# Layer-norm square sums moved to VectorE, reciprocals read from PSUM, and neighbour sums queued ahead of the tail steps

## The chip, the cores and the metric

The kernel runs on one core of one Trainium2 chip. The metric is the device time of one execution in microseconds, as the median of the runs; lower is better. TensorE does matmuls (PE in the profile, its weight loads PEld), VectorE is DVE, ScalarE is ACT, GpSimd is POOL, SyncE is SP. Each engine works through its own queue in the order of the program; between engines there are only semaphores.

## The reference

Four graph layers run one after the other over 16 graphs that share one adjacency matrix of 1024 nodes, with 128 features for each node. An entry of the matrix is set with probability 0.0078, so a node has some 8 neighbours. Layers L0, L2 and L3 are masked attention with 8 heads of 16 features and a feed-forward block; L1 is a graph attention with one score for each edge.

```python
# L0, L2, L3
scores = einsum('bnhd,bmhd->bhnm', h @ Wq, h @ Wk) / 4, -inf where adj == 0
x = h + softmax(scores) @ (h @ Wv) @ Wo + bo
x = layer_norm(x) * ln1_g + ln1_b
y = relu(x @ W1 + b1) @ W2 + b2
x = layer_norm(x + y) * ln2_g + ln2_b
# L1
h = x @ W;  e = leaky_relu(h @ a_src (of the row) + h @ a_dst (of the neighbour))
x = layer_norm(softmax(e, -inf where adj == 0) @ h + x)
# layer_norm(v) = (v - mean(v)) * rsqrt(var(v) + 1e-5), over the 128 features
```

## The kernel before

A preparation sorts the nodes by degree and makes lists of neighbours; a dense path for graphs that do not fit the lists is in the program and is not run here. After the preparation the work is 64 **units**: layer (4) by group of 8 graphs (2) by block of 128 nodes (8). A unit has **parts**: in an attention layer a part is up to two gathers from the table of keys and values (`gathered`, L841, indirect DMAs from POOL), five parts in most units and seven in the first block of a group. A unit of L1 has three or four parts of up to four gathers.

For each part of an attention unit VectorE does three passes over some 2048 elements in each partition: P, query times key (`products`, L868); R, the sum over the 16 features of a head (`exponentials`, L891, after which ScalarE takes the exponential, L895); and W, value times exponential (`weighted`, L919). W is for the part before, P and R are for the current one. Then TensorE adds the edges' rows into an accumulator in PSUM (`summed`, L935), two iterations after P, and this gives P's buffer free (tile `pr`, four buffers). The last part of a unit (input `qx`) has half the elements, so its P and R are short.

After a unit's last part, `divided` (L963) adds up the exponentials in a PSUM bank (`den`), ScalarE copies that to `both`, VectorE takes the reciprocal (L973) and multiplies it into the accumulator for each half of the 8 graphs (L976, tile `o`). This starts two **tails**, one for each half block of 4 graphs (`attention_tail` L631, `graph_tail` L674), the second one step behind the first. A tail is a generator: each `yield` ends a step. An attention tail goes: transpose `o`; multiply by Wo into PSUM (`yps`); normalise; transpose with gain and shift (`turned`, L600, tile `x`); W1 and relu (L655, L659); W2 into PSUM (L664, L668); normalise; transpose; project to the next layer's keys and values, or put out.

`normed` (L575) is the normalisation. The mean has been taken out by the weights, so only the square sum is needed. In one step ScalarE squares each of the 4 graphs' 128 columns out of PSUM and accumulates each one's sum in `total` (L580, 4 instructions with an accumulator); in the next, POOL raises `total` to the power -0.5 (L586); in the next, ScalarE scales each graph's columns (L589).

The order is written out by hand (`manual_schedule`, the loop from L1055). An iteration is one part: P; `others()`; `summed` of two parts back, and at a unit's end the first half of `divided`; R and the exponential; `others()`; W of the part before and a gather; at a unit's end all tail steps that are left and the second half of `divided`; `others()`. One `others()` (L1003) advances all tails by a step, as often as a pace says, and one step of preparing the next unit (`fronts`: queries, L823 and L831; or loads). The pace is STEPS (15) or GRAPH_STEPS (8) over the number of calls in the unit. So what stands in `others()` ahead of the exponential in the program stands ahead of it in ScalarE's queue too.

Of the kernel before, what the change touches and what calls it, by code (L numbers as in the profile page):

```python
# [15 lines left out]
AF = mybir.ActivationFunctionType  # L16
ALU = mybir.AluOpType
# [4 lines left out]
D = 128  # L22
# [23 lines left out]
GH = G // HF  # L46
# [59 lines left out]

STEPS = 15
GRAPH_STEPS = 8  # L110
EDGES = 4
AHEAD = 4

# [9 lines left out]
def sparse_path(ctx: ExitStack, tc: tile.TileContext, a: dict, out: bass.AP, flag):  # L123


    nc = tc.nc
# [6 lines left out]
    def bank(shape):  # L133
        return banks.tile(shape, F32, tag="ps", name="ps")
# [22 lines left out]
    root = const.tile([P, 1], F32, name="root")  # L157
# [24 lines left out]
    def gather_buffer():  # L182
        return gathers.tile([P, max(4 * ROW, J * (ROW + G))], F32, tag="e", name="e")
# [391 lines left out]
    def normed(y):  # L575

        z = twos.tile([P, GH, D], F32, tag="o", name="z")
        total = smalls.tile([P, GH], F32, tag="total", name="total")
        for i in range(GH):
            nc.scalar.activation(  # L580
                z[:, i, :], y[:, i, :], AF.Square, scale=D**-0.5, bias=root,
                accum_out=total[:, i : i + 1],
            )
        yield
        rstd = smalls.tile([P, GH], F32, tag="rstd", name="rstd")
        nc.gpsimd.tensor_tensor(rstd, total, power, ALU.pow)  # L586
        yield
        for i in range(GH):
            nc.scalar.activation(z[:, i, :], y[:, i, :], AF.Copy, scale=rstd[:, i : i + 1])  # L589
        return z  # L590
# [178 lines left out]
    def is_attention(u):  # L769
        return LAYERS[units[u][0]][1] is ATTN  # L770
# [157 lines left out]
    def marked(t, chunk, outs, rhss):  # L928

        j, r = chunk  # L930
        for mark, j in (
            [(MARK[t, j, r], j)] if j < J else [(MARK[t, MIX, k], SHARED[t][k]) for k in range(2)]
        ):
            last = (MIX, 0) if j in SHARED[t] else (j, COUNT[t][j] - 1)
            nc.tensor.matmul(  # L935
                outs[32 * j : 32 * j + 32], marks[:, mark, :], rhss,
                start=(r == 0 and chunk[0] != MIX), stop=(chunk == last),
            )
# [24 lines left out]
    def divided(u):  # L963

        l, g, t = units[u]
        heads, d = (H, HD) if is_attention(u) else (1, D)
        den = bank([P, G * heads])
        for n, c in enumerate(sum(PIECES[t], [])):
            marked(t, c, den, exs[u][:, n, :])
        both = smalls.tile([P, 2, G * heads], F32, tag="both", name="both")  # L970
        nc.scalar.copy(both[:, 0, :], den)
        yield
        nc.vector.reciprocal(both[:, 1, :], both[:, 0, :])  # L973
        for h in range(HF):
            o = twos.tile([P, GH, D], F32, tag="o", name="o")
            nc.vector.tensor_tensor(  # L976
                o.rearrange("p g (a d) -> p (g a) d", d=d),
                accums[u][:, h, :].rearrange("p (a d) -> p a d", d=d),
                both[:, 1, h * GH * heads : (h + 1) * GH * heads]
                .rearrange("p (a o) -> p a o", o=1)  # L980
                .to_broadcast([P, GH * heads, d]),
                ALU.mult,
            )
            tails.append((attention_tail if heads > 1 else graph_tail)(l, g, t, h, o))
        n = G * heads
        nc.gpsimd.tensor_tensor(seen[:, :, :n], seen[:, :, :n], both, ALU.add)

# [5 lines left out]
    def advance(gens):  # L993
        for gen in list(gens):
            if next(gen, "end") == "end":
                gens.remove(gen)
# [3 lines left out]
    def idle():  # L1000
        return slow if held[0] or not busy[0] else []

    def others():  # L1003
        pace[0] += pace[1]
        while pace[0] >= 1.0:
            advance(tails)
            pace[0] -= 1.0
        for gens in (fronts or loads or idle(),):
            if not gens:
                continue  # L1010
            got = next(gens[0], "end")
            if got == "end":
                gens.pop(0)
            if got == "idle":
                advance(idle())

    with tc.manual_schedule():
        wide = [gather_buffer() for _ in range(EDGES)]
        setup, entry, weights = graph(wide), at_once(0), load_weights("L0")
        next(setup)  # L1020
        next(weights)
        next(entry)
        more = [weights, load_graph_weights()]
        rest = slots()
        for i, room in enumerate(setup):
            if i == T:
                for gen in more:
                    next(gen)
            if room == "load":
                for _ in loaded(0):  # L1030
                    next(entry, None)
            elif room == "queries":
                for _ in entry:
                    pass
                for _ in queries(0):
                    pass
            elif isinstance(room, str):
                next(rest)
            else:
                for _ in range(room):  # L1040
                    next(entry, None)
        for _ in entry:
            pass
        scratch.close()
        prods = ctx.enter_context(tc.tile_pool(name="prods", bufs=4))
        smalls = ctx.enter_context(tc.tile_pool(name="smalls", bufs=3))
        slow.append(at_leisure(1))
        for i in range(AHEAD - 1):
            gathered(i)
        nc.gpsimd.memset(wide[3], 0.0)  # L1050
        gathered(AHEAD - 1)
        fronts.extend([rest, loaded(1)] + more)
        closing = None
        begun = 0
        for i in range(len(parts) + 2):  # L1055
            here = i < len(parts)
            u = parts[i][0] if here else len(units)
            if here:
                l = units[u][0]
                if i and parts[i - 1][0] != u:  # L1060
                    begun = i
                    if l + 1 < len(LAYERS) and LAYERS[l + 1][1] is ATTN:
                        if units[u][1:] == (0, 1):
                            more = load_weights(LAYERS[l + 1][0])
                            next(more)
                            next(more)
                        if units[u][1:] == (0, 4):
                            next(more, None)
                if is_attention(u):
                    products(i)  # L1070
            others()
            if i > 1:
                summed(i - 2)
                done = parts[i - 2][0]
                if parts[i - 1 : i] == [] or parts[i - 1][0] != done:
                    closing = divided(done)
                    next(closing)
            if here:
                exponentials(i)
            if here and i == begun + 1:  # L1080
                if is_attention(u):
                    shared(u)
                while loads:
                    advance(loads)
                if u + 1 < len(units):
                    fronts.append(queries(u + 1))
                loads.append(loaded(u + 2))
                if units[u + 2 : u + 3] and units[u + 2][0]:
                    advance(loads)
            others()  # L1090
            if 0 < i <= len(parts):
                weighted(i - 1, 0)
                if not is_attention(parts[i - 1][0]):
                    others()
                    weighted(i - 1, 2)
                gathered(i - 1 + AHEAD)
            if closing is not None and here:
                while tails:
                    advance(tails)
                for _ in closing:  # L1100
                    pass
                closing = None
                passes = 3 if is_attention(u) else 4
                steps = STEPS if is_attention(done) else GRAPH_STEPS
                pace[:] = 0.0, steps / (passes * sum(part[0] == u for part in parts) - 1)
            others()
            if i + 1 >= len(parts) or parts[i + 1][0] != u:

                while fronts:
                    advance(fronts)  # L1110
        while tails:
            advance(tails)
        for _ in closing:
            pass
        while tails:
            advance(tails)
# [434 lines left out]
```

## Time and profile before

| | |
|---|---|
| runs | 2607.16, 2613.10, 2613.42 us; median 2613.1 us |
| the profiled execution's own time | 2568.43 us |
| its span from the first to the last instruction | 2566.7 us |
| mean granted TensorE clock | 0.914 |
| DMA moved | 636.07 MB, mean 248 GB/s |

The profile shows one execution. Its page gives the busy time of each engine, the span in 40 slices, and groups of instructions: line, engine, operation, output and inputs by name, shapes, count, busy time in us, mean ns of one, and the idle time of the engine just ahead of them with what ended it. The view of waits sums that idle time by who waited for whom: us in total, times, the longest. The timeline lists instructions by start time with their length; equal instructions that follow each other are one row with their count, and brackets hold the idle time before the row and who ended it. The profiled execution is 44.7 us shorter than the median of the runs.

Counting units by their reciprocal L973, the first stands at 189.8 us, L0 lasts to about 837 us, L1 to about 1182 us, L2 and L3 follow, and the last reciprocal is at 2525.3 us. Unit 42 (L2), from 1656.77 to 1695.74 us, is looked at closely below.

### The profile page before, as it was taken

The numbers are of one execution on the slowest core, as the hardware profiler recorded it, in microseconds if no ns is written. First come the engines' busy times: TensorE is split into PE (matmuls) and PEld (weight loads), VectorE is DVE, ScalarE is ACT, GpSimd is POOL, SyncE is SP. The second block draws the span as 40 slices with busy tenths as digits, with TensorE's granted clock in tenths as the row PEclk, the third lists the DMA queues.
The fourth block names the chain that finished last, engine by engine and source line by source line (L and its number), as shares of the span: only waits on it lengthen the run. The fifth ranks groups of instructions, "written<-read, shape, count | busy, mean of one in ns | idle before, by whom it ended". The sixth has DMA issues, their size and how long they took to land. (4 is left out here: it accounts for less than half of the span.)

```text
span 2566.7 us, 36698 instructions
## 1 busy us (share of the span) xinstructions
PE 2105.7 (82%) x13124; PEld 1297.6 (51%) x13124; DVE 1931.2 (75%) x1470; ACT 1480.3 (58%) x4640; POOL 1454.9 (57%) x978
## 2 busy tenths in 40 slices
PE   6558888788887898888788888988888787788776
PEld 5425655545554554454455554555555444455444
DVE  7887687587878476567887879888797787877781
ACT  3226676566665554455476666666666565556654
POOL 3335555356665688685554556555565565566561
PEclk8679999899988999999899999999999898889898
DMA  7656777567767598888787877778776767576750
GB/s 242 240 178 235 280 274 276 201 229 256 244 246 243 175 338 305 283 308 298 275 280 246 293 254 268 262 264 294 258 262 249 249 215 259 198 245 223 255 191 18
DMA packets 168463, 636.07 MB, mean 248 GB/s; under 512 B 38328, under 2 KB 41144, under 8 KB 119774
## 3 DMA queue, kind: packets, MB, share of 16 engines
q0 software_dynamic: 92672, 485.09, 53.7%
q1 hardware_dynamic: 75600, 148.55, 17.3%
q8 instruction: 105, 1.72, 0.3%
q14 instruction: 86, 0.70, 0.1%
HBM read 603.11 MB, written 92.34 MB: 271 GB/s over the span
## 5 line engine op out<-in xcount | busy, mean ns | idle before, releaser
L856 POOL DMA_INDIRECT e<-table,idx x600 | 961.3, 1602 | 580.0 <-DVE pr L919 355.3
L919 DVE TENSOR_TENSOR pr<-e,ex 128x2048 f32<-128x2048 f32 (+1 forms) x336 | 689.8, 2061 | 161.8 <-ACT ex L895 138.5
L868 DVE TENSOR_TENSOR pr<-e,qr 128x2048 f32<-128x2048 f32 x204 | 461.1, 2260 | 152.5 <-PE acc L935 85.3
L891 DVE TENSOR_REDUCE sc<-pr 128x128 f32<-128x2048 f32 (+1 forms) x252 | 518.5, 2058 | 8.6
L586 POOL TENSOR_TENSOR rstd<-total,power 128x4 f32<-128x4 f32 x224 | 327.8, 1465 | 326.2 <-ACT z L580 312.5
L935 PE MATMUL acc<-pr,marks 128*32 128x512 f32 x2656 | 487.0, 610 | 31.1 <-DVE pr L919 31.1
L580 ACT ACTIVATE z<-yps,root 128x128 f32<-128x128 f32 x896 | 317.7, 376 | 124.1 <-PE yps L668 68.0
L596 PE MATMUL ps<-ident,z 128*128 128x128 f32 x896 | 208.0, 334 | 162.1 <-ACT z L589 161.6
L589 ACT ACTIVATE z<-yps,rstd 128x128 f32<-128x128 f32 x896 | 255.9, 378 | 92.2 <-POOL rstd L586 89.3
L596 PEld LDWEIGHTS ps<-ident,z 128*128 128x128 f32 x896 | 134.0, 157 | 346.1 <-ACT z L589 251.0
L655 PE MATMUL ps<-x,W 128*128 128x512 f32 x384 | 247.9, 781 | 32.3 <-ACT x L600 32.3
L659 ACT ACTIVATE f<-ps,b 128x512 f32<-128x512 f32 x192 | 132.2, 690 | 232.6 <-PE ps L655 232.5
L664 PE MATMUL yps<-W,f 128*128 128x128 f32 x1536 | 256.5, 285 | 11.2 <-ACT f L659 8.5
L538 PE MATMUL ps<-Wkv,xT 128*128 128x256 f32 x768 | 223.4, 425 | 32.4 <-ACT xT L600 26.7
L935 PEld LDWEIGHTS acc<-pr,marks 128*32 128x32 f32 x2656 | 100.5, 110 | 280.2 <-issue 224.8
L664 PEld LDWEIGHTS yps<-W,f 128*128 128x128 f32 x1536 | 211.4, 196 | 56.1 <-ACT f L659 37.2
L831 ACT COPY qr<-ps 128x512 f32<-128x512 f32 x384 | 196.6, 600 | 53.4 <-PE ps L828 52.9
L580 ACT ACTIVATION_READ_ACCUMULATOR z<-yps,root 128x1 f32 x896 | 193.4, 216 | 0.0
L538 PEld LDWEIGHTS ps<-Wkv,xT 128*128 128x128 f32 x768 | 146.1, 208 | 80.3 <-ACT xT L600 44.6
L644 PE MATMUL yps<-Wo,oT 128*128 128x128 f32 x768 | 159.2, 290 | 6.0 <-ACT oT L598 6.0
L645 PE MATMUL yps<-centre,x 128*128 128x128 f32 x768 | 156.6, 286 | 6.4
L542 ACT COPY kv<-ps 128x512 f32<-128x512 f32 x176 | 103.6, 590 | 89.7 <-PE ps L538 86.1
(159 smaller groups left out, 2644.4 us busy)
## 6 DMA issues: line engine op xcount, KB each, us to landing
table<-kv SPq DMA_DIRECT2D x88, 512.0 KB, 10.6
qx<-qr SPq DMA_DIRECT2D x96, 256.0 KB, 9.4
kept<-xT SPq DMA_DIRECT2D x96, 256.0 KB, 5.0
x<-kept SPq DMA_DIRECT2D x48, 512.0 KB, 9.1
e<-table,idx POOLq DMA_INDIRECT x600, 8.1
table<-kv SPq DMA_DIRECT2D x32, 256.0 KB, 11.0
edges<-in_adj SPq DMA_DIRECT2D x8, 512.0 KB, 4.9
spare<-in_x SPq DMA_DIRECT2D x8, 512.0 KB, 6.6
```

The source lines that it names most:

```text
L538: nc.tensor.matmul(ps[:, k, :], x[:, i + k, :], w[LAYERS[l][0], "Wkv"], start=True, stop=True,)
L580: nc.scalar.activation(z[:, i, :], y[:, i, :], AF.Square, scale=D**-0.5, bias=root, accum_out=total[:, i : i + 1],)
L586: nc.gpsimd.tensor_tensor(rstd, total, power, ALU.pow)
L589: nc.scalar.activation(z[:, i, :], y[:, i, :], AF.Copy, scale=rstd[:, i : i + 1])
L596: nc.tensor.transpose(ps[:, i, :], z[:, i, :], ident)
L655: nc.tensor.matmul(ps, p["W1"][:, f * P : (f + 1) * P], x1.rearrange("p g n -> p (g n)"), start=True, stop=True,)
L664: nc.tensor.matmul(ps[:, i, :], f1[:, f, i * P : (i + 1) * P], p["W2"][:, f, :], start=(f == 0), stop=False,)
L856: nc.gpsimd.indirect_dma_start(out=es[i][:, k, :], out_offset=None, in_=tables[l, g][:, :], in_offset=bass.IndirectOffsetOnAxis(ap=idx[:, ...
L868: nc.vector.tensor_tensor(prs[i][0][:, :n, :], es[i][:, :n, :ROW], qx[u].rearrange("p (o c) -> p o c", o=1) if (MIX, 0) in piece else of_p ...
L891: nc.vector.tensor_reduce(sc[:, :n, :], prs[i][0][:, :n, :].rearrange("p k (a d) -> p k a d", d=HD), mybir.AxisListType.X, ALU.add,)
L919: nc.vector.tensor_tensor(prs[i][k0 // 2][:, :m, :].rearrange("p k (a d) -> p k a d", d=d), es[i][:, k0 : k0 + m, base : base + ROW].rearr ...
L935: nc.tensor.matmul(outs[32 * j : 32 * j + 32], marks[:, mark, :], rhss, start=(r == 0 and chunk[0] != MIX), stop=(chunk == last),)
```

## The change

- `normed`: the four squares with an accumulator become one ScalarE instruction over 512 columns, which only squares. One more step is added, and after it VectorE adds up `z` over the features into `total` (128 x 4). The power on POOL comes in the same step as VectorE's sum. STEPS becomes 17 and GRAPH_STEPS 9, for the longer tails.
- `divided`: the reciprocal reads `den` in PSUM. ScalarE's copy of `den` to `both`, which only the check `seen` on POOL still needs, moves to the end.
- The loop: `summed` and the first half of `divided` come before the first `others()` of an iteration, not after it.

Lines of the changed kernel are a few lower: L580 becomes L579 (square), the new VectorE sum is L582, L586 is L584, L589 is L587, L891 is L889, L919 is L917, L935 is L933, L973 is L970, L971 is L982.

```diff
-STEPS = 15
-GRAPH_STEPS = 8
+STEPS = 17
+GRAPH_STEPS = 9
...
         total = smalls.tile([P, GH], F32, tag="total", name="total")
-        for i in range(GH):
-            nc.scalar.activation(
-                z[:, i, :], y[:, i, :], AF.Square, scale=D**-0.5, bias=root,
-                accum_out=total[:, i : i + 1],
-            )
-        yield
+        nc.scalar.activation(z, y, AF.Square, scale=D**-0.5, bias=root)
+        yield
+        yield
+        nc.vector.tensor_reduce(total, z, mybir.AxisListType.X, ALU.add)
         rstd = smalls.tile([P, GH], F32, tag="rstd", name="rstd")
         nc.gpsimd.tensor_tensor(rstd, total, power, ALU.pow)
         yield
...
         both = smalls.tile([P, 2, G * heads], F32, tag="both", name="both")
-        nc.scalar.copy(both[:, 0, :], den)
-        yield
-        nc.vector.reciprocal(both[:, 1, :], both[:, 0, :])
+        yield
+        nc.vector.reciprocal(both[:, 1, :], den)
...
             tails.append((attention_tail if heads > 1 else graph_tail)(l, g, t, h, o))
+        nc.scalar.copy(both[:, 0, :], den)
         n = G * heads
         nc.gpsimd.tensor_tensor(seen[:, :, :n], seen[:, :, :n], both, ALU.add)
...
-            others()
             if i > 1:
                 summed(i - 2)
                 done = parts[i - 2][0]
                 if parts[i - 1 : i] == [] or parts[i - 1][0] != done:
                     closing = divided(done)
                     next(closing)
+            others()
             if here:
                 exponentials(i)
```

## The prediction

> **What bounds the kernel now.** First the page's busy shares: no engine is full, so one must ask what the fullest in-order queue waits for.
>
> ```profile
> PE 2105.7 (82%) x13124; PEld 1297.6 (51%) x13124; DVE 1931.2 (75%) x1470; ACT 1480.3 (58%) x4640; POOL 1454.9 (57%) x978
> ```
>
> Second, VectorE's waits, longest first. These four make 452.7 us. The reader is to see that three of them are ScalarE or TensorE being late, not VectorE being short.
>
> ```profile
> DVE both L973 <- ACT both L971: 152.3, 57, 11.9
> DVE pr L919 <- ACT ex L895: 138.5, 63, 8.2
> DVE pr L868 <- PE acc L935: 99.2, 28, 9.5
> DVE sc L900 <- DMA e<-table,idx: 62.7, 34, 3.9
> ```
>
> Third, the groups that the change touches.
>
> ```profile
> L586 POOL TENSOR_TENSOR rstd<-total,power 128x4 f32<-128x4 f32 x224 | 327.8, 1465 | 326.2 <-ACT z L580 312.5
> L580 ACT ACTIVATE z<-yps,root 128x128 f32<-128x128 f32 x896 | 317.7, 376 | 124.1 <-PE yps L668 68.0
> L580 ACT ACTIVATION_READ_ACCUMULATOR z<-yps,root 128x1 f32 x896 | 193.4, 216 | 0.0
> ```
>
> Fourth, one unit in the timeline. The sequence hardly varies from unit to unit, so I took unit 42 (L2, 38.97 us). VectorE's rows with a wait, and those that are needed below:
>
> ```profile
> 1656.77 0.55 DVE L973 RECIPROCAL both<-both 128x64 f32<-128x64 f32 x1 [1.27 <-ACT both L971]
> ...
> 1665.35 2.29 DVE L868 TENSOR_TENSOR pr<-e,qr 128x2048 f32<-128x2048 f32 x1
> 1667.67 2.29 DVE L891 TENSOR_REDUCE sc<-pr 128x128 f32<-128x2048 f32 x1
> ...
> 1682.91 1.23 DVE L919 TENSOR_TENSOR pr<-e,ex 128x1024 f32<-128x1024 f32 x1 [1.48 <-ACT ex L895]
> 1687.40 2.29 DVE L868 TENSOR_TENSOR pr<-e,qr 128x2048 f32<-128x2048 f32 x1 [3.26 <-PE acc L935]
> ...
> 1695.74 0.55 DVE L973 RECIPROCAL both<-both 128x64 f32<-128x64 f32 x1 [1.52 <-ACT both L971]
> ```
>
> ScalarE in the same unit: the square of the second half block stands behind four copies, and later an exponential and a square stand behind relus that wait for TensorE.
>
> ```profile
> 1667.32 2.05 ACT L831 COPY qr<-ps 128x512 f32<-128x512 f32 x4 [0.89 <-PE ps L828]
> 1669.23 0.40 ACT L580 ACTIVATE z<-yps,root 128x128 f32<-128x128 f32 x1
> ...
> 1672.49 0.78 ACT L600 ACTIVATE x<-ps,ln_b,ln_g 128x512 f32<-128x512 f32 x1 [0.23 <-PE ps L596]
> ...
> 1681.19 0.69 ACT L659 ACTIVATE f<-ps,b 128x512 f32<-128x512 f32 x1 [3.00 <-PE ps L655]
> ...
> 1682.63 0.25 ACT L895 ACTIVATE ex<-sc 128x64 f32<-128x64 f32 x1
> 1682.78 0.36 ACT L580 ACTIVATE z<-yps,root 128x128 f32<-128x128 f32 x1
> ```
>
> So an attention unit is 33 us of VectorE work and some 6 to 9 us of waits, and what sets the waits is the tail: a chain from `o` through two normalisations that takes about 30 us of a 39 us unit.
>
> **What the Trainium skill says.** "VectorE: DVE Perf Modes", the section on the perf-mode tier table, has `tensor_reduce` at 1x whatever the type or memory. The trace agrees: 2.29 us for 2048 elements, 1.22 for 1024. "GPSIMD Engine Reference", Specifications: POOL's SBUF interface is contended by VectorE instructions with two SBUF inputs. The power L586 fits: 1.04 us median, 3.2 at most. "TensorE: Matmul & The Clock Gate", the part on the HAM clock gate: an idle window halves the clock. In unit 42 the first W1 (L655) takes 3.47 us and the second 1.88, and the first comes 2.19 us of idleness later. "Perfetto Trace Analysis", Tensor Engine Instruction: VectorE, ScalarE and POOL are strict FIFO, which every wait above shows.
>
> **The change part by part.**
>
> *Squares.* Gone: 896 squares and 896 accumulator reads, 317.7 + 193.4 = 511 us of ScalarE. Added: 224 squares over 512 columns. The nearest row is the relu L659, PSUM to SBUF with a bias pointer, at 0.69 us: 155 us. ScalarE loses 356 us, but it is 58% busy, so this counts only where a chain gets shorter: after a pair of squares, 13.15 in place of 14.0 us in the unit (below).
>
> *Sums on VectorE.* 224 reductions of 128x512. The line through 2.29 and 1.22 us gives 0.15 + 0.53 = 0.68 us; the bounds are 0.6 and 0.75. That is 152 us on the engine with the fewest gaps, four in an attention unit, 2.7 us.
>
> *The wait it adds.* Each sum waits for its square, and behind it in VectorE's queue stand P, R and W of the next parts, so also the sums on TensorE, the gathers' buffers and everything that ScalarE does after an exponential. The added `yield` is the cover. But the pace is now 17 steps over 14 calls, so two steps fall into one call at the 5th and 10th. The order of the built program shows it: P, sum, sum, R early in the unit, and W, sum, P, sum, R late. I walk through unit 42, in us from the reciprocal's start:
> - Up to the second P as before, 10.9. First sum 10.9 to 11.6: its square (before at 8.2) is ready.
> - Second sum: its square still stands behind the L831 copies, 12.46 (1669.23), so it ends at 13.15. VectorE waits 1.6. Sum to 13.9.
> - R 16.2, W 18.5, short P and R 20.9, W 23.2.
> - ScalarE has the exponential of that R ahead of `x` (L600), so `x` starts at 16.6, where before it was 15.7. The chain from there is unchanged: W1, relu, W2, W1 of the other half, relu, exponential (25.9 before, 26.8 now), square, ending at 27.65.
> - Third sum: VectorE has been ready since 23.2 and waits 4.5. Sum 28.4, P 30.7, fourth sum (square ready at 30.3) 31.4, R 33.7, short W 34.9, P 37.2, R 39.5, W 41.8: 41.9 with the gaps between them, against 38.97.
>
> New waits are 6.1 us, new work 2.7; gone are all three waits of this unit, 1.27 or 1.52 + 1.48 + 3.26 = 6. The net is +2.9.
>
> *Sums first.* The P at 1687.40 waited because its sum stood behind the tail's W2. Put ahead of the tail step it is ready before P comes: -3.26. The step moved, the first `others()`, takes its DMAs with it (key/value tables, kept inputs, outputs, row loads), but `summed` and `divided` put nothing on the SP or POOL queues, so no DMA changes place there. What moves is TensorE's tail work, behind a sum that is gated by W. In the walk TensorE has idle time there.
>
> *Reciprocal from PSUM.* It loses the hop through ScalarE (0.2 us and its queue), and `den` comes a tail step earlier. Reading PSUM: 128x512 from PSUM takes 0.69 us in L976, no more than from SBUF. I count the wait of 1.3 to 1.5 us as gone. The late copy delays `seen` on POOL, with gathers behind it; those wait for W anyway (355.3 us of POOL's idle time), so 0; without that cover 64 x 0.3 = 19 us. `den` also holds one of four PSUM banks longer; 0, at most 64 x 0.3.
>
> *Sum over units.* About 41.9 for an ordinary attention unit after the change. L2's 14 five-part units have a mean of 40.2: +24. L3's 13 have 41.3 (`x` is late there by POOL's power, which now runs beside a reduction with one input): +8. L0, where loading the other group's rows hinders the chain too, +1 each: +15. Five seven-part units are nearly full of VectorE work (43.5 us): +2.5 each, 12. L1: 88% DMA share from 900 to 1160 us, and sums' 1.4 us fall into waits for gathers; the reciprocal comes up to 1 us earlier: -5. The total is +54: 2568.4 + 54 = 2622 in the profiled execution. The median of the runs is 44.7 above it: 2613.1 + 54 = 2667.
>
> The same by totals: waits removed at most 152 + 138 + 99 = 390; added 152 + 48 x 6.1 = 445; +55.
>
> **Rivals.**
> *A, faster.* The square arrives in time because the chain with less ScalarE work ahead of it runs earlier than in my walk, so the sums wait only 1.6 us in a unit. For it: ScalarE loses a quarter of its work. Against it: the late squares wait for W1 on TensorE, not for ScalarE. With the exponential's wait half gone it gives -(152 + 99 + 69) + 152 + 48 x 1.6 = -91: 2522 on the median. It decides once new waits fall below (390 - 152) / 48 = 5 us in a unit with all old ones gone.
> *B, much slower.* POOL's power runs beside P or W and takes 2 to 3.2 us, the scale and `x` come 1.9 later in each normalisation, and VectorE waits that much longer: +54 + 48 x 1.9 = +145: 2758.
> *C, hidden.* Gains and losses meet within 0.3% (8 us): 2613. If the first W1 runs at full clock, 1.6 us go from the walk in L2 and L3, 54 - 43 = +11.
>
> **How the numbers follow.** Forecast 0.62, A 0.17, B 0.11, C 0.10. 0.3% is about what a measurement of this kernel can tell from no change. From these, faster 0.17, same 0.10, slower 0.73. The range takes in C, half of A's way for bounds of the unknown costs (sum 0.6 us, waits 1 us shorter: -66 from 2667 is 2600), and most of B: 2595 to 2745.
>
> **What would show it.** Right: idle time ahead of the new sum of some 200 to 300 us, put down to ScalarE's square, with two waits a unit; the waits of L868 for the accumulator and of the reciprocal nearly gone; VectorE near 2080 us busy; ScalarE near 1125. Wrong: sums that wait under 100 us in all, or a shorter span with the exponential's wait gone. B would show as powers of over 2 us and waits of L587 for POOL.

## The result, and the profile after

| | before | after |
|---|---|---|
| runs side by side, median | 2610.4 us (2607.16 to 2613.42, 4 runs) | 2688.18 us (2687.28 to 2692.57, 4 runs) |
| ratio | | 1.0302, 95% interval 1.0282 to 1.0321 |
| the profiled execution's own time | 2568.43 us | 2692.57 us |
| its span | 2566.7 us | 2690.8 us |
| granted TensorE clock | 0.914 | 0.884 |

The change makes the kernel 3.0% slower, by 78 us at the medians. The two profiled executions lie 124 us apart, because the one of before is 42 us below its median and the one of after is not. What is read off the two profiles below adds up to 124, not to 78; that the other 46 us come from the change is not shown.

The page's busy line first. VectorE has gained 122.8 us of work and its idle time has hardly moved: 2566.7 - 1931.2 = 635.5 us before, 2690.8 - 2054.0 = 636.8 us after.

```profile
PE 2175.2 (81%) x13124; PEld 1339.5 (50%) x13124; DVE 2054.0 (76%) x1694; ACT 1300.0 (48%) x3072; POOL 1468.3 (55%) x978
```

That invites the reading "the new work costs its own time, and the waits are as they were". VectorE's waits, longest first, show that they are not: some three quarters of them now stand in one place.

```profile
DVE total L582 <- ACT z L579: 464.8, 130, 13.5
DVE sc L898 <- DMA e<-table,idx: 39.1, 24, 3.0
DVE pr L866 <- DMA e<-table,idx: 28.8, 21, 9.5
DVE both L970 <- PE ps L538: 11.1, 4, 3.2
DVE both L970 <- PE ps L933: 10.1, 4, 4.7
```

The 152.3 us of the reciprocal for ScalarE's copy, the 138.5 us of W for the exponential and the 99.2 us of P for the accumulator are gone from the head of the list; one wait of 464.8 us stands there. The groups that answer to those shown of before:

```profile
L584 POOL TENSOR_TENSOR rstd<-total,power 128x4 f32<-128x4 f32 x224 | 334.5, 1496 | 293.7 <-DVE total L582 284.5
L579 ACT ACTIVATE z<-yps,root 128x512 f32<-128x512 f32 x224 | 155.0, 693 | 139.1 <-PE yps L666 75.6
L582 DVE TENSOR_REDUCE total<-z 128x4 f32<-128x512 f32 x224 | 152.7, 683 | 479.2 <-ACT z L579 464.8
```

The new instructions cost what was forecast, 0.69 us a square and 0.68 us a sum, and POOL's power takes 1.496 us on average for 1.465. The third row's last part is the matter: 479.2 us of idleness just ahead of the sums.

Unit 42 again, in VectorE's timeline of after. It begins with its reciprocal at 1730.91 and ends with the next at 1772.22, 41.31 us; the walk gave 41.9.

```profile
1740.80 2.29 DVE L866 TENSOR_TENSOR pr<-e,qr 128x2048 f32<-128x2048 f32 x1 [1.23 <-DMA e<-table,idx]
1743.01 0.68 DVE L582 TENSOR_REDUCE total<-z 128x4 f32<-128x512 f32 x1
1744.13 0.69 DVE L582 TENSOR_REDUCE total<-z 128x4 f32<-128x512 f32 x1 [0.44 <-ACT z L579]
...
1758.78 0.69 DVE L582 TENSOR_REDUCE total<-z 128x4 f32<-128x512 f32 x1 [4.98 <-ACT z L579]
1759.38 2.28 DVE L866 TENSOR_TENSOR pr<-e,qr 128x2048 f32<-128x2048 f32 x1
```

The third sum waits 4.98 us (4.5 in the walk), and the P behind it starts at once, with no wait for the accumulator. The second sum waits 0.44 us (1.6 in the walk), since VectorE came late to it: the P two instructions before had waited 1.23 us for a gather, which the walk did not have. What the third sum waits for is in ScalarE's timeline of the same time:

```profile
1752.74 0.78 ACT L598 ACTIVATE x<-ps,ln_b,ln_g 128x512 f32<-128x512 f32 x1 [0.17 <-PE ps L594]
1756.41 0.69 ACT L657 ACTIVATE f<-ps,b 128x512 f32<-128x512 f32 x1 [2.88 <-PE ps L653]
1757.27 0.69 ACT L657 ACTIVATE f<-ps,b 128x512 f32<-128x512 f32 x1 [0.17 <-PE ps L653]
1757.85 0.25 ACT L893 ACTIVATE ex<-sc 128x64 f32<-128x64 f32 x1
1758.00 0.68 ACT L579 ACTIVATE z<-yps,root 128x512 f32<-128x512 f32 x1
```

TensorE had written the square's input at about 1755.5 (the last L666 of that half starts at 1755.12 and takes 0.39). The square starts 2.5 us later, because the other half's two relus stand ahead of it in ScalarE's queue and wait for W1. VectorE then stands behind ScalarE, which stands behind TensorE.

### The profile page after: what moved, and what is told of

It is laid out like the page before. It is cut to its first block, busy times and chain, and to the rows that moved or that the text cites. A ratio compares the mean times of both kernels' runs of the same rounds, so it can differ in the third digit from the quotient of the medians.

```text
span 2690.8 us, 35362 instructions
## 1 busy us (share of the span) xinstructions
PE 2175.2 (81%) x13124; PEld 1339.5 (50%) x13124; DVE 2054.0 (76%) x1694; ACT 1300.0 (48%) x3072; POOL 1468.3 (55%) x978
## 5 line engine op out<-in xcount | busy, mean ns | idle before, releaser
L854 POOL DMA_INDIRECT e<-table,idx x600 | 945.1, 1575 | 730.2 <-DVE pr L917 547.5
L917 DVE TENSOR_TENSOR pr<-e,ex 128x2048 f32<-128x2048 f32 (+1 forms) x336 | 688.0, 2056 | 6.4 <-ACT ex L905 2.9
L933 PE MATMUL acc<-pr,marks 128*32 128x512 f32 x2656 | 519.2, 638 | 41.5 <-DVE pr L917 40.7
L889 DVE TENSOR_REDUCE sc<-pr 128x128 f32<-128x2048 f32 (+1 forms) x252 | 517.6, 2054 | 5.6
L582 DVE TENSOR_REDUCE total<-z 128x4 f32<-128x512 f32 x224 | 152.7, 683 | 479.2 <-ACT z L579 464.8
L584 POOL TENSOR_TENSOR rstd<-total,power 128x4 f32<-128x4 f32 x224 | 334.5, 1496 | 293.7 <-DVE total L582 284.5
L653 PE MATMUL ps<-x,W 128*128 128x512 f32 x384 | 260.2, 815 | 83.3 <-ACT x L598 83.3
L587 ACT ACTIVATE z<-yps,rstd 128x128 f32<-128x128 f32 x896 | 254.7, 371 | 121.7 <-POOL rstd L584 121.1
L594 PEld LDWEIGHTS ps<-ident,z 128*128 128x128 f32 x896 | 141.6, 166 | 306.6 <-ACT z L587 205.0
L933 PEld LDWEIGHTS acc<-pr,marks 128*32 128x32 f32 x2656 | 105.5, 115 | 306.8 <-issue 245.2
L538 PE MATMUL ps<-Wkv,xT 128*128 128x256 f32 x768 | 215.6, 426 | 42.1 <-ACT xT L598 36.8
L579 ACT ACTIVATE z<-yps,root 128x512 f32<-128x512 f32 x224 | 155.0, 693 | 139.1 <-PE yps L666 75.6
L642 PE MATMUL yps<-Wo,oT 128*128 128x128 f32 x768 | 169.7, 306 | 6.0 <-ACT oT L596 6.0
L643 PE MATMUL yps<-centre,x 128*128 128x128 f32 x768 | 165.8, 300 | 6.0
```

Source lines behind the costliest of these rows:

```text
L538: nc.tensor.matmul(ps[:, k, :], x[:, i + k, :], w[LAYERS[l][0], "Wkv"], start=True, stop=True,)
L594: nc.tensor.transpose(ps[:, i, :], z[:, i, :], ident)
L653: nc.tensor.matmul(ps, p["W1"][:, f * P : (f + 1) * P], x1.rearrange("p g n -> p (g n)"), start=True, stop=True,)
L854: nc.gpsimd.indirect_dma_start(out=es[i][:, k, :], out_offset=None, in_=tables[l, g][:, :], in_offset=bass.IndirectOffsetOnAxis(ap=idx[:, ...
L889: nc.vector.tensor_reduce(sc[:, :n, :], prs[i][0][:, :n, :].rearrange("p k (a d) -> p k a d", d=HD), mybir.AxisListType.X, ALU.add,)
L917: nc.vector.tensor_tensor(prs[i][k0 // 2][:, :m, :].rearrange("p k (a d) -> p k a d", d=d), es[i][:, k0 : k0 + m, base : base + ROW].rearr ...
```

## The experiments

Theory L: late squares hold VectorE's queue, so the cost is the wait ahead of the sum and what queues behind it. Rival O: the sums, put first, hold TensorE's tail back. Rival W: only VectorE's added work counts. From the second set on also rival P: the extra step and the faster pace are the cost. Each set ran on another chip: the kernel before took 2606.89 us as the median of its runs beside the first set, 2575.53 beside the second and 2579.29 beside the third. Expectations in microseconds were made against some 2610, so the ratios are what is compared. A ratio of one set held against one of another, or against the changed kernel's 1.0302, takes for granted that a ratio carries over from chip to chip; no changed kernel was timed in two sets. Where the argument rests on it, two kernels of the same set are compared as well.

### One part at a time

`e1_no_squares`: the changed kernel without the part on the squares.

```diff
-STEPS = 17
-GRAPH_STEPS = 9
+STEPS = 15
+GRAPH_STEPS = 8
...
-        nc.scalar.activation(z, y, AF.Square, scale=D**-0.5, bias=root)
-        yield
+        for i in range(GH):
+            nc.scalar.activation(
+                z[:, i, :], y[:, i, :], AF.Square, scale=D**-0.5, bias=root,
+                accum_out=total[:, i : i + 1],
+            )
         yield
-        nc.vector.tensor_reduce(total, z, mybir.AxisListType.X, ALU.add)
```

> The changed kernel with the old squares (ScalarE accumulates, 15 and 8 steps): sums first and reciprocals from PSUM are kept. Theory L (late squares: VectorE's queue stands still because the new sum waits for a square at the end of the tail's chain): with no sum in VectorE's queue the waits for the accumulator (99 us) and the reciprocal (152 us) go and nothing takes their place, so it is faster than the kernel before, 2400 to 2540 us. Rival O (order: sums first hold TensorE's tail work back, and that is what costs): not faster than before, 2610 to 2690 us.

Measured: 2557.75 us, ratio 0.9830 (0.9792 to 0.9869). Faster, so O falls; but by less than L had in numbers, and the wait for the accumulator, which L had as gone, is still 94.9 us (99.2 before).

`e2_squares_only`: the kernel before with the reverse of that diff.

> The kernel before with the new squares alone (one ScalarE pass, sums on VectorE, 17 and 9 steps). Theory L: slower than the whole change, because the waits of the reciprocal come on top: 2690 to 2770 us, with some 400 us or more of waits ahead of the new sum. Rival O: the sums on VectorE fall into the waits that were there, 2600 to 2660 us. Rival W (only VectorE's added work counts, 152 us, less what falls into waits): 2650 to 2690 us.

Measured: 2670.46 us, ratio 1.0249 (1.0208 to 1.0291). The number is W's, below L's; the wait ahead of the new sum is 404.3 us, as L had it. The parts do not add up: this one times the other two (`e1_no_squares`) gives 1.0249 x 0.983 = 1.007, where all three together give 1.030.

`e3_sums_first_only`: the kernel before with the loop's new order alone.

```diff
-            others()
             if i > 1:
                 summed(i - 2)
...
                     next(closing)
+            others()
             if here:
```

> The kernel before with the sums ahead of the first tail step alone. Theory L: the 99 us of waits for the accumulator go and the reciprocal's wait shrinks; 2470 to 2570 us. Rival O: 2610 us or more.

Measured: 2545.58 us, ratio 0.9788 (0.9749 to 0.9827). As L had it, and the fastest kernel of this study but for `e6_sum_no_wait`, which leaves work out.

`e4_recip_only`: the kernel before with the reciprocal from PSUM alone.

```diff
-        nc.scalar.copy(both[:, 0, :], den)
         yield
-        nc.vector.reciprocal(both[:, 1, :], both[:, 0, :])
+        nc.vector.reciprocal(both[:, 1, :], den)
...
+        nc.scalar.copy(both[:, 0, :], den)
         n = G * heads
```

> The kernel before with the reciprocal read from PSUM alone, and the copy moved behind. All theories: the reciprocal's wait loses the hop through ScalarE, 64 times 0.3 us, a little more where the copy stood behind other work; 2560 to 2605 us. If the reciprocal's wait of 152 us stays but goes to TensorE by name, it was TensorE's lateness and not the copy.

Measured: 2589.37 us, ratio 0.9945 (0.9924 to 0.9967). VectorE's waits for the reciprocal in this kernel, and in the next fence those of sums first alone:

```profile
DVE both L972 <- PE ps L935: 121.2, 46, 11.7
DVE both L972 <- PE ps L538: 27.3, 6, 7.1
```

```profile
DVE pr L919 <- ACT ex L895: 156.0, 52, 10.8
DVE pr L868 <- PE acc L935: 88.8, 25, 9.1
DVE both L973 <- ACT both L971: 80.2, 34, 9.2
```

The reciprocal from PSUM still waits: 148.5 us in these two rows, now by the name of TensorE, and 183.4 us by all names, for 159.3 before. The copy was late because its sum was. Sums first does halve that wait (152.3 to 80.2), by putting the sum of the exponentials ahead of the tail's matmuls. It leaves the wait that the prediction expected it to remove: P waits 88.8 us for the accumulator, for 99.2. In unit 42 of this kernel it is the same 3.26 us as before:

```profile
1674.22 2.29 DVE L868 TENSOR_TENSOR pr<-e,qr 128x2048 f32<-128x2048 f32 x1 [3.26 <-PE acc L935]
```

In TensorE's timeline of this kernel that sum starts at 1672.26, still right behind the second half's W2: that tail step comes from an earlier call and not from the one that the sum was moved past.

### The wait or the work

After the first set the wait and the work were not told apart: the changed kernel's idle time was unchanged in sum, and W's number had fitted once. Two kernels take away one each, a third takes the sums away and keeps the pace, a fourth adds cover.

`e5_short_sum`: the wait kept, most of the work taken away.

```diff
-        nc.scalar.activation(z, y, AF.Square, scale=D**-0.5, bias=root)
+        nc.scalar.activation(z, y, AF.Square, scale=16**-0.5, bias=root)
...
-        nc.vector.tensor_reduce(total, z, mybir.AxisListType.X, ALU.add)
+        nc.vector.tensor_reduce(total, z[:, :, :16], mybir.AxisListType.X, ALU.add)
```

> The changed kernel, with VectorE summing the squares of only 16 of the 128 features (Square's scale is 16**-0.5 for it), so 7/8 of the summing work is left out; the instruction, its place and its wait on ScalarE's square stay. Theory L (late squares hold VectorE's queue): the 224 sums shrink from 0.68 to some 0.2 us, about 105 us of VectorE work goes, but much of it turns into a longer wait at the same place, since the square is no earlier; 2620 to 2670 us, and over 450 us of wait ahead of the sum. Rival W (only VectorE's added work counts): the time falls by all of those 105 us, 2570 to 2605. Rival P (the extra step and the faster pace cost the time, not the wait or the work): no change, 2670 to 2700.

Measured: 2635.23 us, ratio 1.0219 (1.0187 to 1.0251). Against the changed kernel's 1.0302 that is 0.8%, some 21 us for 100 us of VectorE's work (busy 1953.8 us for 2054.0). By the ratio W falls; L and P, whose ranges meet at 1.023, are not told apart here. The group of the sums shows a longer wait in place of work:

```profile
L582 DVE TENSOR_REDUCE total<-z 128x4 f32<-128x64 f32 x224 | 48.6, 218 | 516.3 <-ACT z L579 515.4 <-POOL seen L984 0.7
```

`e6_sum_no_wait`: the work kept, the wait taken away.

```diff
-        nc.vector.tensor_reduce(total, z, mybir.AxisListType.X, ALU.add)
+        nc.vector.tensor_reduce(total, over_graphs(ident), mybir.AxisListType.X, ALU.add)
```

> The changed kernel, with VectorE's sum reading a constant (the identity, read for each graph, so every sum is 1) in place of the squares; the normalisation's dependence on the data is left out. The sum's work stays, its wait on the square goes; the power, the scale and what follows no longer wait for the square either. L: most of the 465 us of waiting ahead of the sum goes, and a part of it comes back at other places (exponential, gathers); 2500 to 2610. W: 2660 to 2700. P: 2670 to 2700.

Measured: 2466.31 us, ratio 0.9572 (0.9544 to 0.9599), 7% less than the changed kernel with the same VectorE work (2049.8 us busy). W and P fall. The gain is an upper bound on what the wait costs, since the power no longer needs the square either, which shortens each normalisation. A part of the waits of before comes back:

```profile
DVE pr L917 <- ACT ex L893: 81.2, 32, 9.4
DVE pr L866 <- PE acc L933: 77.6, 27, 6.5
```

`e9_pace_only`: the old squares with the new steps and pace.

```diff
-        nc.scalar.activation(z, y, AF.Square, scale=D**-0.5, bias=root)
+        for i in range(GH):
+            nc.scalar.activation(
+                z[:, i, :], y[:, i, :], AF.Square, scale=D**-0.5, bias=root,
+                accum_out=total[:, i : i + 1],
+            )
         yield
         yield
-        nc.vector.tensor_reduce(total, z, mybir.AxisListType.X, ALU.add)
```

> The changed kernel, with the four squares with an accumulator of the kernel before in place of one square and VectorE's sum, but with the added step between square and power and the pace 17/9 kept. L: the hold on VectorE goes, and what is left is one more step in each normalisation: 2545 to 2610, near the 2558 of the kernel with 15/8. W: the same, since no VectorE work is added. P: the step and the pace are the cost: 2640 to 2700.

Measured: 2549.78 us, ratio 0.9895 (0.9862 to 0.9928). P falls again. With the same steps, pace, order and reciprocal, the exchange of accumulators for sums alone costs 1.0302 / 0.9895, 4.1%, if the ratio carries over. Within this set, and so on one chip, the wait with a third of the work (e5) takes 2635.23 us for 2549.78 here, 3.4% more, where the work that is left is 48.6 us, 1.9%.

`e7_more_cover`: one more step between the square and the sum.

```diff
-STEPS = 17
-GRAPH_STEPS = 9
+STEPS = 19
+GRAPH_STEPS = 10
...
         yield
         yield
+        yield
         nc.vector.tensor_reduce(total, z, mybir.AxisListType.X, ALU.add)
```

> The changed kernel with one more step between the square and VectorE's sum, pace 19/10. L: the sums come later in VectorE's queue and wait less, 150 to 300 us in place of 465, but the chain of a tail gets two steps longer and the last of it runs into the unit's end; 2600 to 2690. W: no change, 2670 to 2700. P: slower by as much as the first added step cost, 2700 to 2760.

Measured: 2557.33 us, ratio 0.9937 (0.9904 to 0.9970). By the ratios one line gives back 3.5%, with the VectorE work unchanged (busy 2048.9 us). In the same set it stands 0.3% above the kernel with no sums at all (2549.78 us), so with this cover nearly the whole price of the sums is gone. L had this sign but a smaller gain, and a somewhat smaller wait than the one that is left:

```profile
L583 DVE TENSOR_REDUCE total<-z 128x4 f32<-128x512 f32 x224 | 152.4, 680 | 316.4 <-ACT z L579 309.6 <-POOL rstd L585 3.8 <-ACT z L588 2.7
```

So the wait ahead of the sum isn't a price by itself: these 316 us stand in place of waits elsewhere, and VectorE idles 502.8 us in all, for 618.5 with no sums. In unit 42 of this kernel the third sum has moved behind the P that it used to hold back:

```profile
1686.55 2.29 DVE L867 TENSOR_TENSOR pr<-e,qr 128x2048 f32<-128x2048 f32 x1
1692.48 0.69 DVE L583 TENSOR_REDUCE total<-z 128x4 f32<-128x512 f32 x1 [3.64 <-ACT z L579]
1693.08 2.28 DVE L890 TENSOR_REDUCE sc<-pr 128x128 f32<-128x2048 f32 x1
```

### Which sums

`e10_sums_at_first`: accumulators again in the second normalisation of the attention tail only. `normed` gets an argument that chooses between the two forms, both with two steps, and the second call has it off:

```diff
-        z = yield from normed(ps)
+        z = yield from normed(ps, sums=False)
```

> The changed kernel with the four squares with an accumulator put back in the second normalisation of the attention tail only; the first one and L1's keep VectorE's sums. Steps and pace stay at 17/9. In the trace of the changed kernel the sums of the second normalisation (96 of 224) hold 330 of the 480 us of waiting, those of the first 117, L1's 32. Theory L (late squares hold VectorE's queue): nearly all of the cost goes with these 330 us; 0.985 to 1.005 of the kernel before. Rival W (VectorE's added work counts): 96/224 of the cost goes; the kernel with the same steps and no sums has 0.9895, the changed one 1.030, so 1.01 to 1.02.

Measured: 2578.9 us, ratio 1.0003 (0.9985 to 1.0022).

`e11_sums_at_second`: the same line in the first normalisation and in L1's.

> The reverse: VectorE's sums stay in the second normalisation of the attention tail only (96 of 224), the first and L1's take the accumulators again; 17/9. L: the long waits stay; 1.01 to 1.03 of the kernel before. W: 1.00 to 1.012, as 96/224 of the cost stays.

Measured: 2651.13 us, ratio 1.0269 (1.0248 to 1.0291). VectorE's longest wait in e10 and in e11:

```profile
DVE total L590 <- ACT z L580: 151.0, 71, 10.1
```

```profile
DVE total L590 <- ACT z L580: 444.4, 64, 19.6
```

Above the 0.9895 of no sums at all, 128 sums in the first normalisations and L1's cost 1.1% and 96 in the second ones 3.8%. L holds in both, W in neither: a sum behind W1, relu and W2 costs over four times as much as one of the others, 96 of which stand behind Wo and 32 in L1. On the one chip of this set, e11 is 72 us slower than e10 with 32 sums fewer.

### Two on the way to a better version

`e12_cover_old_recip`: `e7_more_cover` with the reverse of the diff of `e4_recip_only`.

> The kernel with one more step ahead of the sum (19/10), with the reciprocal read from ScalarE's copy as in the kernel before. Sums first with the old reciprocal took 0.9788 of the kernel before, with the reciprocal from PSUM 0.983. If the bank that the late copy holds costs something, this one is 0.3 to 0.8% faster than the 0.9937 of the same kernel with the reciprocal from PSUM: 0.985 to 0.991. If the reciprocal gains by skipping ScalarE, it is slower: 0.995 to 1.005.

Measured: 2562.45 us, ratio 0.9934 (0.9915 to 0.9953), for 0.9937 with the reciprocal from PSUM. Neither side was met: here, where the reciprocal reads from makes no difference that these runs tell. In the first set, without the new squares, the one from PSUM was a little slower: sums first take 2545.58 us with the old reciprocal (e3) and 2557.75 with the one from PSUM (e1), 0.5% more.

`e13_two_more`: two more steps in place of one, STEPS 21 and GRAPH_STEPS 11.

> The changed kernel with two more steps in place of one between the square and VectorE's sum, pace 21/11. L: the wait ahead of the sum goes on shrinking (480 us with the change's cover, 316 with one more step), to under 220 us; the time is 0.975 to 0.995 of the kernel before unless the longer chain takes it back. W: no less than 0.9937, the kernel with one more step, since the work is the same.

Measured: 2579.0 us, ratio 1.0008 (0.9993 to 1.0023). A miss for L: the wait ahead of the sum stays at 318.5 us, for 316.4 with one more step, and the time is 0.7% longer, which W's bound of 0.9937 allows. Each step raises the pace too, so two steps fall into one call more often, and a step is worth less than a call of cover. Whether that is all that keeps the wait up isn't settled.

## Why the prediction was right, and where it was not

The forecast of 2667 us stands beside 2688.18: slower, by 78 us at the medians where it had 54, and within its range.

*Late squares on VectorE's queue: right, and shown.* With the work and without the wait the kernel is faster than before (e6); with all the work and one more step of cover it is 0.3% above the kernel with no sums (e7 and e9), with the wait and a third of the work 3.4% (e5). The normalisation with the longest wait in the walk, the one of the third sum, is where most of the cost lies (e10, e11). That an engine takes its queue strictly in order is shown not by every wait, as the prediction says, but by ScalarE's in unit 42 before: the exponential at 1682.63 had its input from the short R by 1674.60, and ScalarE stood idle for 3.00 us ahead of the relu in front of it.

*Square and sum, 0.69 and 0.68 us: right.* In the queue a sum takes less, 0.60 us from the third sum's start to P's, since records of successive instructions overlap; so VectorE has 122.8 us more busy time and not 152.

*ScalarE's work: mis-sized.* The step subtracted 317.7 + 193.4 us. These records overlap: ScalarE's busy time fell by 180.3 us, so the old squares and their reads held the engine for some 155 + 180 = 335 us, 1.50 us for a set of four. ScalarE stands at 1300 us and not near 1125. This did not reach the time, since the walk used its own gain of 0.85 us for a pair of squares.

*New waits, 6.1 us a unit: mis-sized.* By tracing each sum's square to what wrote its input, the second normalisation's 96 sums wait 330 us in the 48 attention units, 6.9 each unit (4.5 in the walk), the first one's 117 us, 2.4 each (1.6), and L1's 32. In sum 479 us for 48 x 6.1 = 293, and outside the 200 to 300 us that were named as a sign. L0 has most for a unit, 173 us in 16.

*Waits gone, at most 390: also mis-sized, in the other direction.* The idle time ahead of W fell by 155.4 us, ahead of P by 129.5, of the reciprocal by 134.8 and of the scores that wait for gathers by 21.4: 441 us. Another 37 us went elsewhere, 26 of them ahead of VectorE's last instruction; 20 us of the sums' waits now stand after the last unit's reciprocal instead.

*The total, +55: too small by more than half between the profiles, near at the medians in part by luck.* Measured, the sum is 123 + 479 - 478 = 124 us; the forecast's was 152 + 293 - 390. The waits were mis-sized by 186 us and the other terms took back 117. That 54 stands so near to 78 is because the medians lie 46 us closer together than the two profiles do; no run says on which terms these 46 us fall.

*"Put ahead of the tail step it is ready before P comes: -3.26": wrong in its cause.* Sums first leaves this wait nearly as it is (e3: 88.8 us in all, 3.26 in unit 42). In the changed kernel VectorE has by then waited at the third sum, and in e2, where the sums are not first, the wait for the accumulator is gone as well (0.3 us). Of the waits, sums first shrinks only the reciprocal's by much, for a gain of 2.1%. In the changed kernel that gain is not seen: with the squares' part in place, adding the other two parts moves the ratio from 1.0249 to 1.0302. That fits edits that went for the same idle time, which could be won only once: in e2 the reciprocal's wait is down to 92.1 us without them.

*Reciprocal, "1.3 to 1.5 us as gone": wrong in its cause too.* Its wait was TensorE's and stayed (e4, 183.4 us in all). Alone it gained 0.5%; with sums first it gained nothing (e12) or cost 0.5% (e1 beside e3).

*The sum over units: mis-sized.* The walk's end, 41.9 us, was taken for the length of every unit and set against each layer's mean of before, 40.2 us in L2. But unit 42, at 38.97, was shorter than that mean, and after the change it is the shortest of L2. Unit 42 grew by 2.3 us; all of L2, between the reciprocals that bound it, by 46.6 us (700.8 for 654.2), 2.9 a unit, where 24 and two seven-part units at 2.5 were forecast. The walk's difference, +2.9, carried to all 16 units of L2, would have given 46. L3 grew by 37.0 for a forecast of 8 and 5, L0 by 24.5 for some 17, and L1, forecast at -5, by 14.6 (359.6 for 345.0; its bounds before are 856.3 and 1201.3 us by the reciprocals, not 837 and 1182). Part of this may be the 46 us that only the profiles show. In e4, whose time is within 0.6% of the kernel before in its set, L2 takes 654.9 us, as before (654.2), but L3 675.8 and L1 356.4: L2's growth stands, L1's is in doubt.

*Rivals.* B was not it: POOL's power averages 1.496 us for 1.465, 6.7 us in all. It does run slowly beside P and W. The Trainium skill says in "GPSIMD Engine Reference", Specifications, that VectorE instructions with two SBUF inputs contend with POOL for the SBUF interfaces, and the trace agrees: the 40 powers that begin while a long P runs take 3.01 us, the 28 that begin beside a W 1.98 on average, the one beside a short P 1.11, and the other 155 at most 1.05. But before it did so too: 24 beside a long P at 2.61 us, 44 beside a W at 2.08. A needed waits under 5 us a unit and they were 9.3. With one more step of cover the change does become faster than the kernel before, by 0.6%, with 316 us of waits: A's sign was a matter of one `yield`, though neither its size nor its threshold is met there.

What stays open: why the profiled execution of before ran 42 us under its median. It may have been on another chip, since the kernel before took 2575.53 and 2579.29 us on those of the later sets, but no run shows it. Open too is what keeps the sum's wait at some 316 us with more cover; and what a square placed ahead of the other half's relus would bring, which was not tried.

## What to carry to other kernels

Before work is moved to the in-order engine that carries the main loop, follow the chain that feeds it to the point where the new instruction would stand: if the input comes late, all that is queued behind waits too, and the price can be this holding up and not the work (here 3.4% with a third of the work, and 0.3% with all of it and one more step of cover). Neither an unchanged sum of idle time nor the length of the new wait tells the price; take away the wait and the work one at a time. When one repeat of a loop is walked through, carry its difference to the others, not its length.

## What the runs showed of the hardware

- A set of four ScalarE squares with accumulators over 128x128 holds the engine for 1.50 us, while its records sum to 2.37: each read of 216 ns lies in part beside the next square (in unit 42 before, a read from 1665.18 to 1665.39 us and the next square from 1665.27). One square over 128x512 takes 0.69 us.
- VectorE's sum over 128x512 takes 683 ns and over 128x64 218 ns, so by a straight line through the two a fixed part of some 0.15 us, as the estimate from the longer rows had it.
- In the trace of after, POOL's power over 128x4 takes 1.00 to 1.05 us where it begins with VectorE idle or reducing, and 3.01 us where it begins beside a multiply of two SBUF inputs of 128x2048 (P).
- TensorE is busy 69.5 us longer after the change with the same 13124 matmuls, at a granted clock of 0.884 for 0.914. The Trainium skill says in "TensorE: Matmul & The Clock Gate", in the part on the HAM clock gate, that after an idle window the clock is half of the full one. The trace of before agrees: in unit 42 the granted clock is 0.50 from 1673 to 1676 us, behind idle times of 2.19 and 0.87 us, and 1.00 from 1677; the four matmuls of the first W1 take 3.47 us there and those of the second 1.88. That waits on VectorE make the chain that they wait for slower in this way is likely but not shown. The matmul of W1 takes 815 ns on average after, 781 before and 733 in e6, which waits least; but in e13 it takes 677 at a clock of 0.922, with 318 us of waits ahead of the sums. How much of the 78 us the clock is, no run here separates.
